# Running 16 early expert tiles between the pieces of the second image's routing, in a two-layer MetaFormer kernel

## The chip, the cores and the metric

The kernel runs on one core of a Trainium2 chip. The time is the device time of one execution in microseconds (us). An execution of the program also leaves a profile: the busy time of each engine, the waits between them, and the clock that TensorE was granted. In the profile PE is TensorE, PEld its weight loads, DVE VectorE, ACT ScalarE, POOL GpSimd and SP SyncE, which here issues most DMAs. L784 means line 784 of the kernel.

## What is computed

The input is two images of 256 channels and 56 x 56 pixels. Two layers follow one another, each a token mixer and a mixture of experts with a residual around both. Layer 0 mixes by 7 x 7 window attention, layer 1 by two ternary 3 x 3 convolutions with batch normalisation over both images. The part that matters here is layer 1 after its convolutions:

```python
x = x + relu(out1 + out2)             # out2: second convolution, normalised over both images
t = tokens(x)                         # 2 * 56 * 56 = 6272 tokens of 256 numbers
n = layer_norm(t)
logits = n @ gate_w + gate_b          # 8 experts
top2_vals, top2_idx = top_k(softmax(logits), 2)
for each expert e:                    # 256 -> 512 -> 256
    y = gelu(n @ W1[e] + b1[e]) @ W2[e] + b2[e]
    acc += weight of e for the token * y
x = t + acc
```

All of it is float32, and the output has the shape of the input.

## The kernel before

Each image is cut into 7 strips of 8 pixel rows, 448 tokens each; STRIPS lists the 14 of them, image 0's first. A strip's tokens are held as 4 groups of 112 tokens.

**Routing of layer 1.** `residual(i)` loads the strip's kept input (`back`), adds the two convolutions' results on DVE (L2071), rectifies on ACT (L2074), turns the strip from channels to tokens with 8 PE transposes (L2083) and adds `back` on DVE (L2087). `norm` takes the mean and variance per token on DVE (L705, L707), a square root on ACT (L712), scales into `u` on ACT (L726), turns `u` back with 8 PE transposes (`pu`, L770) and two ACT copies (`ut`, L775), and multiplies by the gate (`pl`, 16 matmul records, L784). `settle` takes a batch of one or two strips: it finds each token's two best experts by some 15 small DVE steps (L811 to L860) with a rank count on PE (`rk`, L843 to L846), which gives each token a row in its expert's stretch of a table `xs` in DRAM. POOL then scatters the tokens there, one indirect DMA for 112 tokens and one of the two choices (L870), so 8 for a strip. All these functions are generators, and `in_order` advances them step by step, so that two or three strips are under way at once. DVE, PE, ACT and SP take their work in the order in which it is written there; POOL's is not in that hand-written order.

**Tiles.** An expert's rows are worked off in tiles of 256 rows. `tiles(part)` computes on DVE, from the counts, which expert and rows each tile has. Part 0 holds tiles that are known to be full once the first FIRST[1] = 10 strips are placed: EARLY[1] = (2 * 448 * 10 - 8 * 255) // 256 = 27 of them. Part 1 holds the other full tiles, 41 full ones in all, and part 2 the 23 half tiles of 128 rows. From the ninth place on (MIX = 8) half tiles are mixed among the full ones. The early tiles' rows may be read while late strips are still being scattered; `fence` makes SP wait until the early ones are written.

**The expert loop.** `experts_in_order` runs over 64 tiles j. SP issues the rows of tile j + 4 and the weights of tile j + 3 (1154 KB). `turn(j + 2)` transposes rows on PE (L1073) and copies them on ACT (L1077). `first(j + 1)` makes 4 PSUM tiles `ph` (L1105), each followed by a Gelu on ACT (L1112). `second(j)` makes `py` (L1122), DVE adds the bias into `y` (L1130), and POOL scatters the tile's rows into `ys` (L1132), two indirect DMAs for a full tile. `gates`, the softmax weights of all tokens, is advanced by one step after each tile.

In the kernel before, `in_order` runs all 14 strips, and only then the loop starts its first tile:

```python
plan, n_full = tiles(1, in_order(), True)
plans1.append(plan)
plans1.append(tiles(2, n_full, True))
nc.sync.value_load(fences[0])
route_ps.close()
...
experts1.send((tp1, ps1))
```

Behind the expert loop the two rows of each token are gathered from `ys`, weighted and added, and the result is turned back to channels.

Layer 0 has the same two parts. There the loop over tiles already runs beside the routing of the last four strips, by a function `beside` that is called once per tile.

Of the kernel before, what the change touches and what calls it, by code (L numbers as in the profile page):

```python
# [10 lines left out]
F32 = mybir.dt.float32  # L11
# [44 lines left out]
NEVER = -3e38  # L56
U_BUFS = (4, 6)

# [574 lines left out]
def metaformer(ctx: ExitStack, tc: tile.TileContext, a: dict, out: bass.AP, flag):  # L633
# [3 lines left out]
    dram = ctx.enter_context(tc.tile_pool(name="dram", bufs=3, space=DRAM))  # L637

    def disjoint(inst, group, others):
# [96 lines left out]
    def routing(layer, wp, tp, ps):  # L736
# [18 lines left out]
        def norm(i, src, late=False):  # L755
# [20 lines left out]
            if layer == 0:  # L776
                eng.tensor_tensor(src, src, u, ALU.add)
                nc.sync.dma_start(x_mid[i], src)
                yield
            lg = lgs[:, i * NTT : (i + 1) * NTT, :]  # L780
            pl = ps.tile([TT, NTT, E], F32, tag="pl" if layer else "aux", name="pl")
            for t in range(NTT):
# [239 lines left out]
    def experts_in_order(layer, FF, plans, ys, wp, at_tile):  # L1022
# [13 lines left out]
        live = {}  # L1036

        def planned(j):
# [27 lines left out]
        def turn(j):  # L1066
            d = live[j]
            _, held, name, n = planned(j)
            gp = blocks_of(j)
            pt = ps.tile([P, KC, G], F32, tag="pt", name="pt", bufs=2 if layer else 1)  # L1070
            for k in range(KC):
                for i in range(gp):
                    nc.tensor.transpose(  # L1073
                        pt[:, k, i * P : (i + 1) * P], d["xg"][:, i, k * P : (k + 1) * P], ident
                    )
            d["ut"] = tp.tile([P, KC, G], F32, tag="ut", name="ut")
            nc.scalar.copy(d["ut"][:, :, : gp * P], pt[:, :, : gp * P])  # L1077
# [73 lines left out]
        for j in range(len(tiles)):  # L1151
# [66 lines left out]

    BATCHES = [[0], [1], [2], [3], [4, 5], [6, 7], [8, 9], [10, 11], [12, 13]]

# [94 lines left out]
    with ExitStack() as st:  # L1315
# [324 lines left out]
        x_all = None  # L1640
        X, XT, pad, sums = {}, {}, [], []
        mid = ctx.enter_context(ExitStack())
        pads = mid.enter_context(ExitStack())
        wq_held = ExitStack()

        def routed_all():
# [21 lines left out]

            cp = pads.enter_context(tc.tile_pool(name="pads", bufs=1, reuse_waits="tile"))
            for b in range(B):  # L1670
                t = cp.tile([P, HC, KC, WC], F32, tag=f"pad{b}", name=f"pad{b}")
# [3 lines left out]
                nc.gpsimd.memset(t[:, 1 : HC - 1, :, WC - 1 : WC], 0.0)  # L1675
                pad.append(t)
            mid.enter_context(wq_held)
# [32 lines left out]
    with mid:  # L1710
# [336 lines left out]
        with ExitStack() as both:  # L2047
# [9 lines left out]
            route_ps = ExitStack()  # L2057
            ps = route_ps.enter_context(
                tc.tile_pool(name="route_ps1", bufs=2, space=PSUM, reuse_waits="tile")
            )  # L2060

            def residual(i):

                b, s = STRIPS[i]
                r = X[b, s]
                nr = tp.tile([P, KC, NT], F32, tag="nr", name="nr")
                back = tp.tile([TT, NTT, C], F32, tag="back", name="back")
                nc.sync.dma_start(back, x_mid[i])
                for o in range(KC):
# [9 lines left out]
                    )  # L2079
                pt = ps.tile([TT, NTT, C], F32, tag="pt", name="pt")  # L2080
                for t in range(NTT):
                    for k in range(KC):
                        nc.tensor.transpose(  # L2083
                            pt[:, t, k * P : (k + 1) * P], nr[:, k, t * TT : (t + 1) * TT], ident
                        )
                yield
                nc.vector.tensor_tensor(XT[b, s][:TT], pt, back, ALU.add)  # L2087

# [11 lines left out]

            def in_order():


                n = len(STRIPS)
                jobs = {}
                ready = iter(())
                for i in range(n + 2):
# [3 lines left out]
                    finish(ready)  # L2111
                    if not plans1 and FIRST[1] - 1 in sent:
                        plan, n_early = tiles(0)
                        plans1.append(plan)
                        fence()
                    if young == 0:
                        next(jobs[young])
                    if i < n:
                        jobs[i] = strip(i)
                        next(jobs[i])  # L2120
                        if i == n - 1:

                            next(experts1)
                    if young > 0 and young in jobs:
# [19 lines left out]
            experts1 = experts_in_order(1, 2 * C, plans1, ys[1], wp1, lambda j: next(gating, None))  # L2144
            with tc.manual_schedule(engines=ENGINES):
                plan, n_full = tiles(1, in_order(), True)
                plans1.append(plan)
                plans1.append(tiles(2, n_full, True))

                nc.sync.value_load(fences[0])  # L2150

                route_ps.close()
                pads.close()
                tp1 = both.enter_context(tc.tile_pool(name="moe_t1", bufs=2, reuse_waits="tile"))
                ps1 = both.enter_context(
                    tc.tile_pool(name="moe_ps1", bufs=2, space=PSUM, reuse_waits="tile")
                )
# [133 lines left out]
```

## Time and profile before

| | us |
|---|---|
| median of 3 runs | 1854.04 |
| lowest and highest run | 1850.1, 1854.89 |
| the profiled execution | 1852.05 |
| its span (what the profile covers) | 1850.1 |
| PE busy | 1530.3 (83%) |
| DVE busy | 979.4 (53%) |
| ACT busy | 696.1 (38%) |
| POOL busy | 655.1 (35%) |

Times in the views are counted from the span's start. The layer 1 routing begins at about 1182 us and the first expert tile's second half at about 1399; the last stage, from about 1780 on, gathers and writes out. A view by windows gives the busy time of each engine in a stretch, the clock granted to PE as a share of full speed, and the DMA's share and rate. In a list of waits, the engine named behind the arrow is the one whose signal came last; "remote" and "another core or an unknown queue" mean that the profile found no engine of the core for it. In a timeline each line is one instruction or a run of like ones: start, duration, engine, line, operation, and in brackets the idle time before it and what ended that.

### The profile page before, as it was taken

Reading aid. Unit: us, or ns where it says so; the run is one execution under the profiler, and the core shown is the slowest. Engines: PE = TensorE matmul, PEld = TensorE weight load, DVE = VectorE, ACT = ScalarE, POOL = GpSimd, SP = SyncE. Lnnn points to the kernel's source line nnn. Section 1 sums busy time; section 2 is a strip of 40 time slices with the busy share of each in tenths; the row PEclk is TensorE's granted clock in tenths of the full one; section 3 lists DMA queues with packets and bytes.
Section 4 is the critical chain, followed back from the end, with each engine's and each line's share of the span. In section 5 each row is a group of like instructions: output and inputs, shape, how many; then the busy total and the mean of one; then the engine's idle time right before and its main releaser. Section 6 shows DMA issues by size and latency. Waiting matters only on the chain.

```text
span 1850.1 us, 25838 instructions
## 1 busy us (share of the span) xinstructions
PE 1530.3 (83%) x8612; PEld 1199.4 (65%) x8612; DVE 979.4 (53%) x2688; ACT 696.1 (38%) x1358; POOL 655.1 (35%) x664
## 2 busy tenths in 40 slices
PE   6999998999778669894899799666348999999963
PEld 3555555555467557783788688555337888888842
DVE  4467566465645337845999788666432111111136
ACT  3454442434333324643444532344213333333312
POOL 3112534335333654442344143164562222222210
PEclk9999988999889879995999899755558999999975
DMA  7022333213267667885551000133544778788758
GB/s 244 22 83 82 113 90 112 62 52 93 60 205 229 230 208 263 307 256 156 158 163 53 1 1 1 40 112 98 170 136 152 270 265 270 262 279 277 274 161 301
DMA packets 91886, 291.77 MB, mean 158 GB/s; under 512 B 20487, under 2 KB 35803, under 8 KB 80416
## 3 DMA queue, kind: packets, MB, share of 16 engines
q1 hardware_dynamic: 66736, 231.79, 40.5%
q0 software_dynamic: 21200, 51.82, 8.0%
q10 hardware_dynamic: 3808, 6.42, 1.0%
q8 instruction: 70, 1.15, 0.3%
q14 instruction: 72, 0.59, 0.1%
HBM read 218.51 MB, written 74.20 MB: 158 GB/s over the span
## 4 chain that ended last, share of the span: by engine, by line
PE 52%; DVE 21%; DMA 8%; issue 7%; another core or an unknown queue 5%; POOL 4%; ACT 3%; SPq 0%; POOLq 0%; ACTq 0%; DVEq 0%
PE ph L1105 14%; PE py L1122 12%; PE av L1486 5%; PE sc L1457 3%; PE pj L1409 3%; DVE x L1191 3%; PE pw L1556 3%; PE pv L1431 3%; PE pl L784 2%; PE pt L1073 2%; DMA got<-ys 2%; DMA out<-o_out 2%; DVE oc L1543 2%; DVE t_stats L705 2%
## 5 line engine op out<-in xcount | busy, mean ns | idle before, releaser
L1105 PE MATMUL ph<-ut,w 128*128 128x256 f32 (+1 forms) x1472 | 320.3, 370 | 28.2 <-issue 20.3
L1130 DVE TENSOR_TENSOR y<-py,w 128x512 f32<-128x512 f32 (+1 forms) x120 | 76.8, 640 | 439.2 <-PE py L1122 379.2
L1122 PE MATMUL py<-w,h 128*128 128x256 f32 x1288 | 298.8, 380 | 0.0
L1105 PEld LDWEIGHTS ph<-ut,w 128*128 128x128 f32 x1472 | 258.2, 200 | 59.8 <-issue 22.4
L870 POOL DMA_INDIRECT xs<-u,pos x224 | 217.1, 969 | 168.0 <-issue 87.0
L1122 PEld LDWEIGHTS py<-w,h 128*128 128x128 f32 x1288 | 244.8, 192 | 33.1
L1132 POOL DMA_INDIRECT ys<-y,dest x136 | 136.3, 1003 | 274.8 <-DVE dest L1080 185.5
L1112 ACT ACTIVATE h<-ph,w 128x256 f32<-128x256 f32 (+1 forms) x368 | 162.3, 447 | 131.2 <-PE ph L1105 82.2
L1476 ACT ACTIVATE ex<-sc 112x476 f32<-112x476 f32 (+3 forms) x224 | 116.7, 570 | 207.8 <-PE sc L1466 174.9
L1077 ACT COPY ut<-pt 128x512 f32<-128x512 f32 (+1 forms) x120 | 65.2, 543 | 302.5 <-PE pt L1073 244.9
L1486 PE MATMUL av<-ex,vals 112*64 112x238 f32 (+3 forms) x896 | 124.1, 397 | 17.8 <-DVE acc L1496 14.3
L1792 PE MATMUL pc<-lo,wq 128*128 128x448 f32 x336 | 132.2, 395 | 6.5 <-DVE lo L1767 6.4
L1496 DVE TENSOR_TENSOR acc<-av,acc 128x238 f32<-128x238 f32 (+3 forms) x224 | 87.8, 407 | 87.5 <-PE av L1486 65.3
L1792 PE MATMUL pc<-hi,wq 128*128 128x448 f32 x336 | 131.7, 394 | 2.0 <-DVE x L1816 1.8
L1132 POOL DMA_INDIRECT ys<-y,to x81 | 82.3, 1016 | 135.0 <-DVE dest L1080 76.4
L1191 DVE SCALAR_TENSOR_TENSOR x<-got,wgt,x 112x256 f32<-112x256 f32 x216 | 102.3, 544 | 30.4 <-DMA got<-ys 30.4
L1935 PE MATMUL pc<-hi,wq 128*128 128x448 f32 (+1 forms) x288 | 104.4, 371 | 15.9 <-ACT hi L1902 9.4
L1935 PE MATMUL pc<-lo,wq 128*128 128x448 f32 (+1 forms) x288 | 103.6, 368 | 0.2 <-DVE lo L1903 0.2
L1457 PE MATMUL sc<-q_im,keys 32*112 32x238 f32 (+3 forms) x896 | 94.3, 427 | 9.5 <-ACT ex L1476 5.7
L1486 PEld LDWEIGHTS av<-ex,vals 112*64 112x64 f32 x896 | 55.9, 141 | 67.7 <-issue 25.2
L1765 POOL TENSOR_TENSOR v<-pad 128x928 f32<-128x928 f32 (+1 forms) x28 | 56.4, 2028 | 99.4 <-DVE lo L1767 49.1
L1073 PE MATMUL pt<-ident,xg 128*128 128x128 f32 x434 | 71.7, 287 | 15.5 <-ACT ut L1077 10.4
(273 smaller groups left out, 2479.7 us busy)
## 6 DMA issues: line engine op xcount, KB each, us to landing
w<-in_L_experts SPq DMA_DIRECT2D x64, 1154.0 KB
w<-in_L_experts SPq DMA_DIRECT2D x56, 641.0 KB
xg<-xs SPq DMA_DIRECT2D x97, 260.0 KB
got<-ys SPq DMA_DIRECT2D x28, 896.0 KB
acc<-in_fresh SPq DMA_DIRECT2D x14, 896.0 KB
xt<-in_x_tok SPq DMA_DIRECT2D x14, 448.0 KB
xr<-in_x_tok SPq DMA_DIRECT2D x14, 448.0 KB
rec<-shares SPq DMA_DIRECT2D x28, 224.0 KB
```

Source lines behind the costliest of these rows:

```text
L870: w = nc.gpsimd.indirect_dma_start(xs[:, :], bass.IndirectOffsetOnAxis(ap=pos[:, j, t0 + t : t0 + t + 1], axis=0), us[t // NTT][:, t % NTT ...
L1073: nc.tensor.transpose(pt[:, k, i * P : (i + 1) * P], d["xg"][:, i, k * P : (k + 1) * P], ident)
L1105: nc.tensor.matmul(ph[:, :g], w1[:, k, f * P : (f + 1) * P], d["ut"][:, k, :g], start=k == 0, stop=k == KC - 1,)
L1112: nc.scalar.activation(d["h"][:, f, :g], ph[:, :g], AF.Gelu, bias=b1[:, f : f + 1])
L1122: nc.tensor.matmul(py[:, i, :], d["h"][:, f, i * P : (i + 1) * P], w2[:, f, :], start=f == 0, stop=f == NF - 1,)
L1132: o = nc.gpsimd.indirect_dma_start(ys[:, :], bass.IndirectOffsetOnAxis(ap=d["to"][:, i : i + 1], axis=0), y[:, i, :], None, bounds_check=T ...
L1191: nc.vector.scalar_tensor_tensor(xt[:, t, :], y[:, t, j, :], wgt[:, j, n : n + 1], xt[:, t, :], ALU.mult, ALU.add)
L1457: nc.tensor.matmul(sc[h // 2][:, h % 2, :nq], keys[g][p, c, tx * TT : (tx + 1) * TT], q_im[p, c, r0:r1, c0:c1], start=True, stop=False,)
L1476: nc.scalar.activation(e[:, :, :nq], sc[j][:, :, :nq], AF.Exp, scale=HD**-0.5)
L1486: nc.tensor.matmul(av[VW * i : VW * (i + 1), :nq], vals[g % 3][:, tx, 2 * c + j, 2 * i : 2 * i + 2, :].rearrange("p a d -> p (a d)"), ex[j ...
L1792: nc.tensor.matmul(pc[:, :NT], wq[:, k, c, dx * C + o * P : dx * C + (o + 1) * P], part[:, :, k, dx : dx + W], start=m == 0, stop=m == 2 * ...
L1935: nc.tensor.matmul(pc[:, : 2 * ns * W], wq[:, k, c, dx * C + o * P : dx * C + (o + 1) * P], part[:, : 2 * ns, k, dx : dx + W], start=m == ...
```

## The change

FIRST[1] goes from 10 to 7, so part 0 is what image 0 fills: EARLY[1] = (2 * 448 * 7 - 8 * 255) // 256 = 16 tiles. `in_order` is split. `early_strips` runs strips 0 to 6 as before, plans part 0 and sets the fence. Then the expert loop starts, and `late_strips`, a generator, runs strips 7 to 13 in small steps, 9 to a strip, which `beside1` takes between the parts of each tile: 2 before `first(j + 1)`, 2 between it and `second(j)`, and 3 after. When its steps are used up, or at the latest after tile 11, parts 1 and 2 are planned. Half tiles are mixed in from the 17th tile on, nearly one to one with the full ones.

To have both under way, PSUM is shared: while the strips run, the routing has 2 banks for all its PSUM tiles (`aux`), and the loop has 1 for `pt`, 3 for `ph` and 2 for `py`; afterwards the loop gets 2, 4 and 2 as before. In late strips the result of the transposes (L2083) is held in two halves, and the add (L2087) is made in two. In SBUF image 0's pad is given up before the tiles start, so the pads become two pools; `nr` has one buffer instead of two and `u` 5 instead of 6. The batches of `settle` are arranged so that none spans both images.

```diff
-U_BUFS = (4, 6)
+U_BUFS = (4, 5)
-FIRST = (10, 10)
+FIRST = (10, 7)
-MIX = 8
...
-                tiles.insert(MIX + q + (NFULL - MIX) * q // NHALF, (2, q))
+                tiles.insert(n0 + q + (NFULL - n0) * q // NHALF, (2, q))
...
-            pt = ps.tile([P, KC, G], F32, tag="pt", name="pt", bufs=2 if layer else 1)
+            pt = ps.tile([P, KC, G], F32, tag="pt", name="pt", bufs=2 if wide(ps) else 1)
...
-                ph = ps.tile([P, 512], F32, tag="ph", name="ph", bufs=4 if layer else 3)
+                ph = ps.tile([P, 512], F32, tag="ph", name="ph", bufs=4 if wide(ps) else 3)
...
+            if layer:
+                at_tile(j, 0)
             if j + 1 < len(tiles):
                 first(j + 1)
+            if layer:
+                at_tile(j, 1)
             second(j)
             if at_tile is not None:
-                at_tile(j)
+                at_tile(*((j, 2) if layer else (j,)))
...
-    BATCHES = [[0], [1], [2], [3], [4, 5], [6, 7], [8, 9], [10, 11], [12, 13]]
+    BATCHES = [[0], [1], [2], [3], [4, 5], [6], [7, 8], [9, 10], [11, 12], [13]]
...
-                nr = tp.tile([P, KC, NT], F32, tag="nr", name="nr")
+                nr = tp.tile([P, KC, NT], F32, tag="nr", name="nr", bufs=1)
...
-                nc.vector.tensor_tensor(XT[b, s][:TT], pt, back, ALU.add)
+                xt = XT[b, s][:TT]
+                for at, pt in halves:
+                    nc.vector.tensor_tensor(xt[:, at], pt, back[:, at], ALU.add)
...
+            def late_strips():
+
+                sending = iter(())
+                young = None
+                for i in range(FIRST[1], len(STRIPS) + 1):
+                    job = strip(i) if i < len(STRIPS) else iter(())
+                    steps = iter(())
+                    for q in BATCHES:
+                        if q[-1] == i - 1 and i > FIRST[1]:
+                            steps = settle(q)
+                    for at in range(9):
+                        if at in (0, 2, 3):
+                            next(job, None)
+                        if at in (1, 4, 5) and young is not None:
+                            next(young, None)
+                        if at == 5:
+                            next(job, None)
+                        if at >= 6:
+                            next(steps, None)
+                        next(sending, None)
+                        yield
+                    for _ in sending:
+                        yield
+                    sending, young = steps, job
+                for _ in sending:
+                    yield
...
+            def beside1(j, part):
+                nonlocal route
+                if route is None:
+                    if part == 2:
+                        next(gating, None)
+                    return
+                done = object()
+                for _ in range((2, 2, 3)[part]):
+                    if next(route, done) is done:
+                        break
+                else:
+                    if j < EARLY[1] - ROWS_AHEAD - 1 or part < 2:
+                        return
+                    for _ in route:
+                        pass
+                route = None
+                plan, n_full = tiles(1, n_early, True)
+                plans1.append(plan)
+                plans1.append(tiles(2, n_full, True))
+                late_ps.close()
...
+            experts1 = experts_in_order(1, 2 * C, plans1, ys[1], wp1, beside1)
+            route = late_strips()
             with tc.manual_schedule(engines=ENGINES):
-                plan, n_full = tiles(1, in_order(), True)
-                plans1.append(plan)
-                plans1.append(tiles(2, n_full, True))
-
+                n_early = early_strips()
+                next(experts1)
                 nc.sync.value_load(fences[0])
```

More of the change, by code (lines that the diff above doesn't have):

```diff
@@ L637, in metaformer, with __init__, tile @@
     dram = ctx.enter_context(tc.tile_pool(name="dram", bufs=3, space=DRAM))
+    class Banks:
+        def __init__(self, pool, wide=False):
+            self.pool, self.wide = pool, wide
+        def tile(self, *args, **kw):
+            return self.pool.tile(*args, **kw)
     def disjoint(inst, group, others):
@@ L779, in norm @@
                 yield
+            elif i >= FIRST[1]:
+                yield
             lg = lgs[:, i * NTT : (i + 1) * NTT, :]
-            pl = ps.tile([TT, NTT, E], F32, tag="pl" if layer else "aux", name="pl")
+            pl = ps.tile([TT, NTT, E], F32, tag="pl" if layer and ps.wide else "aux", name="pl")
             for t in range(NTT):
@@ L1036, in experts_in_order, with wide @@
         live = {}
+        def wide(ps):
+            return isinstance(ps, Banks) and ps.wide
         def planned(j):
@@ L1640, in metaformer @@
         x_all = None
-        X, XT, pad, sums = {}, {}, [], []
+        X, XT, pad, sums = {}, {}, {}, []
         mid = ctx.enter_context(ExitStack())
-        pads = mid.enter_context(ExitStack())
+        pads = [mid.enter_context(ExitStack()) for _ in range(B)]
         wq_held = ExitStack()
@@ L1667, in routed_all @@
                 X[b, s] = x_all[:, i, : KC * NT].rearrange("p (k n) -> p k n", n=NT)
-            cp = pads.enter_context(tc.tile_pool(name="pads", bufs=1, reuse_waits="tile"))
-            for b in range(B):
+            for b in reversed(range(B)):
+                cp = pads[b].enter_context(
+                    tc.tile_pool(name=f"pads{b}", bufs=1, reuse_waits="tile")
+                )
                 t = cp.tile([P, HC, KC, WC], F32, tag=f"pad{b}", name=f"pad{b}")
@@ L1675, in routed_all @@
                 nc.gpsimd.memset(t[:, 1 : HC - 1, :, WC - 1 : WC], 0.0)
-                pad.append(t)
+                pad[b] = t
             mid.enter_context(wq_held)
@@ L2057, in metaformer @@
             route_ps = ExitStack()
-            ps = route_ps.enter_context(
-                tc.tile_pool(name="route_ps1", bufs=2, space=PSUM, reuse_waits="tile")
+            ps = Banks(
+                route_ps.enter_context(
+                    tc.tile_pool(name="route_ps1", bufs=2, space=PSUM, reuse_waits="tile")
+                ),
+                True,
             )
@@ L2079, in residual @@
                     )
-                pt = ps.tile([TT, NTT, C], F32, tag="pt", name="pt")
+                if i >= FIRST[1]:
+                    yield
+                halves = []
                 for t in range(NTT):
+                    if i < FIRST[1] and not t:
+                        pt = ps.tile([TT, NTT, C], F32, tag="pt", name="pt")
+                        halves.append((slice(0, NTT), pt))
+                    elif i >= FIRST[1] and not t % 2:
+                        pt = ps.tile([TT, 2, C], F32, tag="aux", name="pt")
+                        halves.append((slice(t, t + 2), pt))
+                    at = halves[-1][0].start
                     for k in range(KC):
                         nc.tensor.transpose(
-                            pt[:, t, k * P : (k + 1) * P], nr[:, k, t * TT : (t + 1) * TT], ident
+                            pt[:, t - at, k * P : (k + 1) * P],
+                            nr[:, k, t * TT : (t + 1) * TT],
+                            ident,
                         )
                 yield
-                nc.vector.tensor_tensor(XT[b, s][:TT], pt, back, ALU.add)
+                xt = XT[b, s][:TT]
+                for at, pt in halves:
+                    nc.vector.tensor_tensor(xt[:, at], pt, back[:, at], ALU.add)
             def strip(i):
@@ L2099, in fence, with early_strips @@
                 fences.append(some)
-            def in_order():
-                n = len(STRIPS)
+            def early_strips():
+                n = FIRST[1]
                 jobs = {}
@@ L2111, in in_order @@
                     finish(ready)
-                    if not plans1 and FIRST[1] - 1 in sent:
-                        plan, n_early = tiles(0)
-                        plans1.append(plan)
-                        fence()
                     if young == 0:
@@ L2120, in in_order @@
                         next(jobs[i])
-                        if i == n - 1:
-                            next(experts1)
                     if young > 0 and young in jobs:
@@ L2139, in in_order @@
                 finish(ready)
-                return n_early
+                plan, n_early = tiles(0)
+                plans1.append(plan)
+                fence()
+                return n_early
+            def late_strips():
[19 more added lines that the diff above has]
+                    for _ in sending:
+                        yield
+                    sending, young = steps, job
+                for _ in sending:
+                    yield
@@ L2142, in metaformer @@
             plans1, fences = [], []
             gating = gates()
-            experts1 = experts_in_order(1, 2 * C, plans1, ys[1], wp1, lambda j: next(gating, None))
-            with tc.manual_schedule(engines=ENGINES):
-                plan, n_full = tiles(1, in_order(), True)
+            def beside1(j, part):
[15 more added lines that the diff above has]
+                plan, n_full = tiles(1, n_early, True)
@@ L2147, in metaformer @@
                 plans1.append(plan)
                 plans1.append(tiles(2, n_full, True))
+                late_ps.close()
+                ps1.pool = late_ps.enter_context(
+                    tc.tile_pool(name="moe_ps1", bufs=2, space=PSUM, reuse_waits="tile")
+                )
+                ps1.wide = True
+            experts1 = experts_in_order(1, 2 * C, plans1, ys[1], wp1, beside1)
+            route = late_strips()
+            with tc.manual_schedule(engines=ENGINES):
+                n_early = early_strips()
+                next(experts1)
@@ L2150, in metaformer @@
                 nc.sync.value_load(fences[0])
                 route_ps.close()
-                pads.close()
+                pads[0].close()
+                late_ps = both.enter_context(ExitStack())
+                ps.pool = late_ps.enter_context(
+                    tc.tile_pool(name="late_ps1", bufs=2, space=PSUM, reuse_waits="tile")
+                )
+                ps.wide = False
                 tp1 = both.enter_context(tc.tile_pool(name="moe_t1", bufs=2, reuse_waits="tile"))
-                ps1 = both.enter_context(
-                    tc.tile_pool(name="moe_ps1", bufs=2, space=PSUM, reuse_waits="tile")
+                ps1 = Banks(
+                    late_ps.enter_context(
+                        tc.tile_pool(name="early_ps1", bufs=2, space=PSUM, reuse_waits="tile")
+                    )
```

## The prediction

> **What bounds the kernel now.** I first cut the stretch that the change touches into windows by stage (columns: window, its length, then busy us and instruction count of PE, PEld, DVE, ACT and POOL, granted clock, DMA share, GB/s). The last two lines are stages of layer 0, read as models.
>
> ```profile
> core 0: us, PE busy (x) PEld busy (x) DVE busy (x) ACT busy (x) POOL busy (x), PEclk, DMA share, GB/s
> 1182.00:1285.00 103.00, 62.24 (x314) 54.13 (x314) 65.28 (x272) 40.80 (x82) 47.80 (x48) 0.52 0.36 104
> 1285.00:1350.00 65.00, 32.96 (x166) 29.32 (x166) 36.52 (x149) 20.83 (x43) 32.15 (x34) 0.50 0.51 160
> 1350.00:1394.00 44.00, 16.80 (x69) 13.66 (x68) 11.85 (x58) 4.62 (x8) 29.19 (x31) 0.58 0.34 110
> 1452.00:1600.00 148.00, 148.00 (x812) 132.49 (x811) 22.40 (x74) 55.84 (x130) 40.34 (x41) 1.00 0.81 272
> ...
> 585.00:685.00 100.00, 70.05 (x350) 59.07 (x349) 38.54 (x147) 28.69 (x56) 62.16 (x64) 0.88 0.67 219
> 720.00:830.00 110.00, 99.66 (x484) 85.90 (x484) 79.74 (x198) 53.76 (x100) 52.00 (x51) 0.95 0.83 274
> ```
>
> Layer 1's routing (1182 to 1394) leaves PE idle for 38 to 62% of its windows at a clock of 0.50 to 0.58; its experts (from 1399) are PE alone, 148 of 148 us at 1.00. Putting tiles into the routing's gaps looks worth much. Next, in the chain of waits, the end of the routing:
>
> ```profile
> 1352.61 15.98 another core or an unknown queue
> ...
> 1379.62 9.28 another core or an unknown queue
> ...
> 1398.95 3.45 PE py L1122 x16
> ...
> 1402.84 3.46 PE ph L1105 x16
> 1406.29 3.45 PE py L1122 x16
> ```
>
> The first second half of a tile (py) starts at 1398.95; from there a full tile takes 7.34 us (1402.84 to 1410.18). In front of it lie waits of no named cause. The list of waits and the timeline show what they go with:
>
> ```profile
> ACT ut L775 <- remote: 46.2, 5, 12.9
> ```
> ```profile
> 1302.73 0.79 PE L846 MATMUL rk<-hots,all_w 112*112 112x56 bf16 x7
> 1303.38 0.99 PE L770 MATMUL pu<-ident,u 112*128 112x112 f32 x4
> ...
> 1308.78 0.94 POOL L870 DMA_INDIRECT xs<-u,pos  x1 [0.30 <-issue]
> 1312.59 0.53 ACT L775 COPY ut<-pu 128x448 f32<-128x448 f32 x1 [12.87 <-remote]
> ```
>
> PE's transposes are done at 1304.4, yet ACT, which waits for them alone, goes on at 1312.59, after POOL's row of scatters (L870, one each 1.25 us, 16 from 1289.7) has ended. The same happens after 10 to 20 scatters in a row: 1229 to 1240, 1273 to 1285, 1352 to 1389. I call it a freeze; the profile names no cause, but PE, ACT, DVE and SP all stop in it. It went with 0.65 to 0.8 scatters per us, not with the 51 POOL instructions in 110 us of the last window above.
>
> **Part by part.** The change is worth what follows from three numbers: when experts start, how long the mixed stage lasts, and how much tile work is then done.
>
> *Earlier start.* FIRST 10 to 7 gives (2 x 448 x 7 - 8 x 255) // 256 = 16 early tiles. Routing stops after strip 6. In the timeline strip 5's logits are added at 1253.43; strip 6, with no strip behind it, follows by 1262, its places by 1267. POOL's scatters of strips 4 and 5 start at about 1259 and those of 6 join on: 24 x 1.25 = 30 us, to 1289. Before, the last scatter ahead of the fence ended at 1334.0 and SP issued the first rows at 1341.92, 7.9 us later; so rows go at 1297. Plan and the first three weight loads (12.6 us for three at 1322.7) lie beside the scatters: nothing, or up to 8 us if the plan's DVE steps are frozen, as they were from 1364 on. Rows 3 us, transposes, copy and one first half at half clock (6.05 us, the 16 matmuls at 1369) and a second: py of tile 0 at about 1315, against 1398.95. **84 us earlier** (75 to 90).
>
> *Length of the mixed stage.* late_strips gives 9 steps for each of 7 strips and 9 to end, and some 5 for the last scatters: 77, at 7 per tile 11.1 tiles. PE's own work: 11.1 x 7.34 = 82 us, and per strip 8 pt transposes (1.2, twice the 0.60 us of four at clock 1.00), 8 pu (1.2), 16 pl (1.74 at 264.98) and the rank matmuls (0.6): 4.7 x 7 = 33. Together 115. What is lost on top:
> - Square roots. L712 stays on ACT, now between Gelus. Layer 0 shows one:
>
> ```profile
> 598.07 1.28 ACT L712 ACT_TABLE_LOAD   x1
> 602.76 0.30 ACT L712 ACTIVATE t_rstd<-t_mv,eps 112x4 f32<-112x4 f32 x1 [3.40 <-DVE t_mv L707]
> 603.55 1.28 ACT L1112 ACT_TABLE_LOAD   x1
> 603.58 0.66 PE L1073 MATMUL pt<-ident,xg 128*128 128x128 f32 x4 [1.54 <-ACT ut L1077]
> ```
>
> ACT is held from 598.07 to 604.8. py went 596.26, 600.15, 606.34: 6.19 where a tile takes 3.89, so 2.3 us lost. 7 x 2.3 = 16.
> - Order. Five of the seven steps of a tile lie together with only 0.6 us of tile work between (after second, before first). There rank waits for DVE's step before it (about 3 us, L811 to L833 at 1298.4 to 1301.8) and pl and pt wait for DVE and ACT to clear the two aux banks (1.22 us, L2087; two copies of 0.53). Laid out by hand over nine tiles I lose 1 to 2 us per strip: 10. With ph in 3 banks and pt in 1, the fourth ph waits for one Gelu (0.47) with 2.6 us to spare: nothing while ACT is free.
> - Freezes. The 16 scatters of two strips come out in 8 steps, 1.1 tiles, with 2 or 3 of ys between: some 23 us of unbroken POOL. About 7 us of PE lost for each of three, 23 with the last strip. Bounds: none (the 720 to 830 window), or the 11 us of each pair seen now and 30 us for the last four strips, 50.
> - Clock. 0.88 in the layer 0 model; 6 us. If 0.5 comes back after freezes, 20.
>
> 16 + 10 + 23 + 6 = 55: 115 + 55 = **170 us**, a PE share of 0.68. The layer 0 window, the nearest row, has 0.70, which gives 164. I take 169, nearer to the itemised sum, since layer 0 has no PE order as tight as this.
>
> The Trainium skill ("ScalarE: Activation LUTs", What ACT_TABLE_LOAD costs) speaks against the change: a switch is about 1.28 us of load and 1.38 us of drain, and unlike functions should be batched. The 14 switches would be 37 us of ACT by it and the total 20 us worse if none of it hid; the row above holds load, drain and wait together. The skill ("SBUF — State Buffer", two separate sides) says that PE and ACT never wait for the port that GpSimd shares; by that a freeze would cost nothing and the total be 23 us better. The timeline above disagrees.
>
> *Work done.* 82 us of tiles need not be run later. So the path grows by 169 - 82 = 87 and starts 84 earlier.
>
> *Handover.* After the last step tiles(1) and tiles(2) go onto DVE in one piece (some 45 steps, about 12 us unfrozen); y of the next tile waits behind them, py has two banks of 7 us, so little of it shows. Rows of tile 16 wait on SP for the late scatters, with the weights of tile 15 queued behind; both are needed two tiles, 15 us, later. New PSUM pool: one drain. **4 us** (0 to 15).
>
> *Half tiles later.* From the 17th on they alternate almost one to one with full ones. A pair moves 2 x 1154 KB of weights, 390 KB of rows and 393 KB of ys in 11.09 us: 278 GB/s against 272 now, with 340 to 408 GB/s seen at 750 to 770. PE never waits there now: nothing (to 8 us if 272 is near the limit).
>
> *Small ones.* The add of L2087 in two halves, two pads, nr in one buffer and u in five: each had its reader done long before (u of strip i - 5 is sent 20 us earlier): nothing.
>
> Sum: -84 + 87 + 4 + 0 = **+7 us**. The profiled execution took 1852.05 us (span 1850.1), 2 below the median of 1854.04: 1859.
>
> **Rivals.** *Scatters thin out (faster).* As steps follow PE's pace, no more than 8 or 10 scatters run unbroken, and freezes go as in the 720 to 830 window; clock stays at 1. Then 115 + 26 = 141: 141 - 82 = 59 and -84 + 59 + 4 = -21, 1831; with the start at its early end (90) and 3 of the handover gone, 1822. It decides once freezes and clock cost under 16 us together instead of 29: then the time is 0.3% below before's. For it: POOL's total is 78 scatters x 1.26 = 98 us in 170. Against: they come in packs of 16.
>
> *POOL sets the pace (much slower).* The last 24 scatters run into one freeze as the last 32 did (1352 to 1394), rows of tile 16 come late: 20 us more freeze and 10 of handover, 1889.
>
> *Weights bound the half tiles.* If 278 GB/s isn't reached beside half tiles, 8 us over the forecast: 1867, and PE waits for w appear after tile 16.
>
> **How the numbers follow.** About 0.3%, 5.6 us, is what a measurement can tell from no change. Forecast, 0.50: of it 0.07 faster, 0.13 within, 0.30 slower. Scatters thin out: 0.30, faster. POOL sets the pace: 0.13; weights: 0.07, both slower. Faster 0.37, same 0.13, slower 0.50. The range goes from the lower rival's end, 1822, to just short of the heaviest, 1885, which leaves out some 0.2. The forecast's own range is 1843 to 1878.
>
> **What would show it.** Right: first py near 1315; the route's scatters in packs of 16 or more, ACT or DVE "remote" waits of 5 us or more at the end of each; 14 table loads more; PE share about 0.7 from there to tile 11; then dense PE at 1.00. Wrong: no remote waits in the mixed stage, or a stage under 150 us (then faster), or PE waits for xg or w after tile 16.

## The result, and the profile after

The changed kernel takes 1880.27 us (1877.35 to 1885.03), the kernel before beside it 1854.47 us (1850.1 to 1859.32): a ratio of 1.0141 [1.0108, 1.0174], slower by 26 us. The profiled execution of the changed kernel took 1885.03 us with a span of 1883.2, against 1852.05 and 1850.1, so the two traces differ by 33 us. The file has grown: L726 is now L733, L775 L782, L793 L802, L870 L879, L1073 L1085, L1077 L1089, L1105 L1117, L1112 L1124, L1122 L1134, L1130 L1142, L1132 L1144, L2087 L2121.

The tile part is framed by the row of `py` from the first tile's start to the last's (count, then least, median and greatest ns, first and last start, shapes). Before, then after:

```profile
L1122 PE MATMUL py<-w,h x840: 379/379/382, 1398.8 to 1777.4; 128*128 128x256 f32 x168
```
```profile
L1134 PE MATMUL py<-w,h x840: 379/379/634, 1311.4 to 1808.5; 128*128 128x256 f32 x168
```

Tile 0 starts 87.4 us earlier; from the first `py` to the last it takes 497.1 us instead of 378.6, which is 118.5 more; the end behind that takes 2.0 more (74.7 against 72.7). -87.4 + 118.5 + 2.0 = +33.1, the difference of the spans. So the whole loss lies in the tile part, and the windows show where in it (same columns as above):

```profile
core 0: us, PE busy (x) PEld busy (x) DVE busy (x) ACT busy (x) POOL busy (x), PEclk, DMA share, GB/s
1182.00:1296.00 114.00, 52.26 (x259) 45.59 (x259) 58.72 (x262) 31.81 (x63) 55.10 (x57) 0.50 0.35 109
1272.80:1298.20 25.40, 0.00 (x0) 0.00 (x0) 0.00 (x0) 0.00 (x0) 13.90 (x16) 0.50 0.68 221
1316.00:1508.00 192.00, 121.97 (x616) 102.45 (x615) 54.64 (x224) 70.05 (x125) 73.08 (x77) 0.79 0.41 138
1508.00:1640.00 132.00, 131.47 (x719) 117.36 (x718) 32.21 (x122) 51.22 (x117) 36.09 (x37) 1.00 0.80 269
```

From 1508 on PE is busy 131.47 of 132 us at full clock: nothing is lost there. In the mixed stage, 1316 to 1508, PE is busy 0.64 of the time at a clock of 0.79. And there is a line that nothing before had: for 25.4 us ahead of tile 0 PE, ACT and DVE do not execute one instruction, while POOL issues the last 15 scatters ahead of the fence, and the fence's own transfer.

The starts of `py` show the mixed stage tile by tile. In us, from tile 0 to tile 11: 10.8, 12.8, 16.6, 16.4, 26.8, 13.7, 30.2, 16.7, 16.0, 30.1, 8.2; together 198.1. Three tiles are twice as long as their neighbours. The timeline of the second shows why (start, duration, engine, line; a cut of it):

```profile
1415.50 0.93 POOL L879 DMA_INDIRECT xs<-u,pos  x1 [0.30 <-issue]
1416.33 2.84 PE L1117 MATMUL ph<-ut,w 128*128 128x256 f32 x12
...
1417.10 0.57 ACT L1089 COPY ut<-pt 128x512 f32<-128x512 f32 x1
...
1419.21 0.93 POOL L879 DMA_INDIRECT xs<-u,pos  x1 [0.30 <-issue]
1420.45 0.98 POOL L1144 DMA_INDIRECT ys<-y,dest  x1 [0.30 <-issue]
...
1431.69 0.94 POOL L879 DMA_INDIRECT xs<-u,pos  x1 [0.30 <-issue]
1432.36 0.19 DVE L802 TENSOR_TENSOR lgs<-pl,gate_b 112x32 f32<-112x32 f32 x1 [15.18 <-remote]
1432.47 0.17 DVE L722 RECIPROCAL t_rstd<-t_rstd 112x4 f32<-112x4 f32 x1
1432.67 0.16 DVE L723 TENSOR_TENSOR t_nmr<-t_nmr,t_rstd 112x4 f32<-112x4 f32 x1
1432.87 2.07 ACT L733 ACTIVATE u<-x,t_nmr,t_rstd 112x256 f32<-112x256 f32 x4 [15.20 <-issue]
```

POOL's row of 18 scatters runs from 1410.55 to 1432.63. PE's last matmul ends at 1419.2, the matmuls (`pl`) that DVE waits for had been done since 1416.5, and DVE goes on at 1432.36: the freeze of the prediction, now beside tiles. The list of waits from 1300 to 1520 has the freezes of all three long tiles (a cut of it):

```profile
DVE lgs L802 <- remote: 31.4, 2, 16.2
...
ACT ut L1089 <- remote: 20.4, 1, 20.4
...
DVE y L1142 <- remote: 18.2, 1, 18.2
```

### The profile page after: what moved, and what is told of

Its sections match the earlier page's. It is cut to its first block, busy times and chain, and to the rows that moved or that the text cites. A ratio compares the mean times of both kernels' runs of the same rounds, so it can differ in the third digit from the quotient of the medians.

```text
span 1883.2 us, 25864 instructions
## 1 busy us (share of the span) xinstructions
PE 1520.2 (81%) x8613; PEld 1186.9 (63%) x8613; DVE 980.7 (52%) x2714; ACT 711.6 (38%) x1372; POOL 652.8 (35%) x664
## 5 line engine op out<-in xcount | busy, mean ns | idle before, releaser
L1117 PE MATMUL ph<-ut,w 128*128 128x256 f32 (+1 forms) x1472 | 327.3, 374 | 42.4 <-ACT h L1124 33.1
L1117 PEld LDWEIGHTS ph<-ut,w 128*128 128x128 f32 x1472 | 261.8, 203 | 78.0 <-ACT h L1124 35.8
L1142 DVE TENSOR_TENSOR y<-py,w 128x512 f32<-128x512 f32 (+1 forms) x120 | 76.8, 640 | 445.7 <-PE py L1134 368.7
L1134 PE MATMUL py<-w,h 128*128 128x256 f32 x1288 | 301.8, 383 | 0.0
L879 POOL DMA_INDIRECT xs<-u,pos x224 | 214.8, 959 | 173.5 <-issue 76.9
L1134 PEld LDWEIGHTS py<-w,h 128*128 128x128 f32 x1288 | 246.1, 193 | 33.5
L1144 POOL DMA_INDIRECT ys<-y,dest x136 | 136.7, 1005 | 311.8 <-DVE dest L1092 128.7
L1124 ACT ACTIVATE h<-ph,w 128x256 f32<-128x256 f32 (+1 forms) x368 | 161.2, 447 | 129.7 <-PE ph L1117 90.3
L1089 ACT COPY ut<-pt 128x512 f32<-128x512 f32 (+1 forms) x120 | 65.0, 542 | 304.2 <-PE pt L1085 252.9
L1144 POOL DMA_INDIRECT ys<-y,to x81 | 82.0, 1012 | 130.0 <-DVE dest L1092 75.8
L1085 PE MATMUL pt<-ident,xg 128*128 128x128 f32 x434 | 73.1, 290 | 45.8 <-DMA xg<-xs 34.9
L1085 PEld LDWEIGHTS pt<-ident,xg 128*128 128x128 f32 x434 | 57.2, 151 | 71.4 <-DMA xg<-xs 33.6
```

The source lines that it names most:

```text
L879: w = nc.gpsimd.indirect_dma_start(xs[:, :], bass.IndirectOffsetOnAxis(ap=pos[:, j, t0 + t : t0 + t + 1], axis=0), us[t // NTT][:, t % NTT ...
L1085: nc.tensor.transpose(pt[:, k, i * P : (i + 1) * P], d["xg"][:, i, k * P : (k + 1) * P], ident)
L1117: nc.tensor.matmul(ph[:, :g], w1[:, k, f * P : (f + 1) * P], d["ut"][:, k, :g], start=k == 0, stop=k == KC - 1,)
L1124: nc.scalar.activation(d["h"][:, f, :g], ph[:, :g], AF.Gelu, bias=b1[:, f : f + 1])
L1134: nc.tensor.matmul(py[:, i, :], d["h"][:, f, i * P : (i + 1) * P], w2[:, f, :], start=f == 0, stop=f == NF - 1,)
L1144: o = nc.gpsimd.indirect_dma_start(ys[:, :], bass.IndirectOffsetOnAxis(ap=d["to"][:, i : i + 1], axis=0), y[:, i, :], None, bounds_check=T ...
```

## The experiments

They came in four sets, each on one chip with the kernel before beside it, and the sets differ in a way that turned out to be the best experiment of all. Each set ran on another chip. The kernel before took 1760.06 us in the first set, 1856.66 in the second, 1758.34 in the third and 1857.66 in the fourth. Where it is near 1760, no trace of any kernel has a "remote" wait; where it is near 1857, all have them. Only ratios within a set are compared below, and traces of the same level.

**First set (kernel before 1760.06): four ways to break up the packs, or the order.**

*Strips settled singly.*

```diff
-    BATCHES = [..., [6], [7, 8], [9, 10], [11, 12], [13]]
+    BATCHES = [..., [6], [7], [8], [9], [10], [11], [12], [13]]
```

> Edit: strips 7 to 12 of the changed kernel are settled one by one instead of in pairs, so a pack has 8 scatters instead of 16. Theory A (packs): the changed kernel's loss beyond the forecast is the three freezes in the mixed stage, which packs of 16 scatters bring about; the three frozen tiles took 26.8, 30.2 and 30.1 us where the other seven took 14.7 on average, 43 us in all. Packs of 8 stay under the 10 scatters after which the freezes set in: no waits of ACT or DVE over 8 us in the mixed stage, 43 us back less some 3 for more DVE steps, so 1838 to 1848 us, faster than the kernel before. Theory B (order): the loss lies in PE's waits for DVE and ACT in the hand-written order (rank counts, square roots with their table switches), and the long gaps are those waits: settling one by one doubles the number of rank waits, so 1880 to 1890 us.

Measured: 1791.02 us, ratio 1.0188 [1.0152, 1.0225]. With nothing frozen in this set, the size of the packs could not be tested. But the loss was there without any freeze.

*Singly, and a step after each scatter.*

```diff
+                    if layer and strips[0] >= FIRST[layer] and not j:
+                        yield
                 yield
```

> Edit: as e1_single, and each of the 8 scatters of a late strip is given a step of its own, so that they are spread over 8 of 9 steps. Theory A: at most 2 or 3 scatters unbroken, so no freeze at all; 0 to 6 us better than e1_single, 1835 to 1845 us. Theory B: as e1_single, 1880 to 1890 us. If e1_single still shows freezes and this kernel none, the length of a pack decides and 8 is already too many.

Measured: 1806.68 us, 1.0263 [1.0235, 1.0292]. The stretch from first to last `py` is 460.7 us against 452.5 of the first: more steps, a longer mixed stage, and what is left over is run in one piece at tile 13 (an interval of 16.5 us where the first has 7.3). The other 10.5 us by which this trace is later, at tile 0, come from ahead of the edit: layer 0's last `py` is at 806.9 against 795.5.

*Without the square roots of the late strips (the root is left out of their normalisation).*

```diff
-            nc.scalar.activation(rstd, mv[:, :, 1], AF.Sqrt, bias=eps[:TT])
+            nc.scalar.activation(rstd, mv[:, :, 1], AF.Identity if root == "late" else AF.Sqrt, bias=eps[:TT])
```

> Edit: in the changed kernel the square root on ACT of the 7 late strips' norm is left out (Identity takes its place, on the same operands), so that ACT changes no table in the mixed stage; each token's logits get a positive factor, so the choice of experts and the tiles stay as they are. Theory A: only the 7 square roots' own cost goes, 7 x 2.3 = 16 us, freezes stay: 1860 to 1868 us. Theory B: ACT's table switches are the main loss, 14 loads and the order around them: 1850 us or less, and the long gaps shrink.

Measured: 1786.2 us, 1.0158 [1.0131, 1.0185]. `py` of tiles 0 to 11 takes 144.2 us; the changed kernel on the third set, the same level, takes 153.2. So the seven roots cost 9 us (the next run, of this set, has the changed kernel's layer 1 and takes 153.6). Without them the stage looks like this:

```profile
1269.30:1413.50 144.20, 121.37 (x648) 104.02 (x647) 60.14 (x242) 53.95 (x115) 69.01 (x73) 0.91 0.55 183
```

*A filler on POOL after each late scatter.*

```diff
+                    if layer and strips[0] >= FIRST[layer]:
+                        nc.gpsimd.tensor_tensor(minus_half, ones[:TT, :NTT], minus_half, ALU.pow)
```

> Edit: in the changed kernel POOL does a small power of about 1.05 us (a step that feeds nothing) after each late scatter, so scatters follow each other after some 2.4 us instead of 1.24, in packs of the same 16. Theory A, rate: freezes come from 0.8 scatters per us; at 0.4 they vanish, some 40 us back, 1835 to 1850 us, unless POOL itself gets late with ys. Theory A, count: freezes come once 10 scatters or so stand in one pack; a pack now lasts 38 us, so they last longer, 1900 us and more. Theory B: POOL is not in it, 1878 to 1885 us.

Measured: 1843.27 us, 1.0484 [1.0452, 1.0516]. It did not test what it was meant to: POOL's order isn't written by hand, and all 56 fillers ran in layer 0. The timeline of POOL:

```profile
507.83 61.23 POOL L887 TENSOR_TENSOR minus_half<-ones,minus_half 112x4 f32<-112x4 f32 x56
```

There they held up the scatters, and with them layer 0's tiles: PE waits 41.85 us for rows there. Its layer 1 is therefore the changed kernel's, with packs of 18, 20 and 28 and nothing frozen: 451.7 us from first to last `py`.

**Second set (kernel before 1856.66): both kernels again, and two changes of size.**

*The changed kernel, unaltered.*

> The changed kernel unaltered, beside the kernel before and the other three of this call on one chip. The four runs so far were on a chip on which the kernel before took 1760.06 us instead of 1854.47, and their traces have no stretch in which PE, ACT and DVE all stand still behind a pack of scatters. Theory A (the stands-still behind the packs, 43 us of the mixed stage, are the excess loss): on a chip without them the ratio to the kernel before is at most 1.00, or with them 1.014 again. Theory B (the order of the steps, PE's waits on DVE and ACT and the lower clock are enough): without stands-still the ratio is still 1.015 to 1.025, since the variants with single strips and without square roots gave 1.019 and 1.016 there.

Measured: 1883.85 us, 1.0118 [1.0072, 1.0163]; the first trace again (tile 0 at 1316.2, 499.9 us of tiles, 25.5 us of standstill ahead of them).

*The kernel before, unaltered.*

> The kernel before unaltered, for its trace beside the changed kernel's on the same chip. Theory A: where the time is near 1760 the waits for another core or an unknown queue, which are on the chain of the routing stage of the first profile, are gone, and that stage (from the end of the convolution at about 1182 to py(0) at 1399 there) is the part that is shorter, by the most of the 94 us. Theory B: all stages are shorter by a common share, 5 per cent, as from a higher granted clock.

One execution, 1866.1 us. Not the level that the expectation spoke of; as in its first trace there are stretches of 4 to 7 us without PE, ACT and DVE in the routing, and tile 0 at 1408.7.

*Twice as many steps per tile.*

```diff
-                for _ in range((2, 2, 3)[part]):
+                for _ in range((4, 4, 6)[part]):
```

> The changed kernel with (4, 4, 6) steps of the late routing per tile in place of (2, 2, 3): the mixed stage has 5.5 tiles instead of 11, each with 14 steps. Theory A (the loss belongs to the strips: their packs, square roots and scatters): the loss is the same per strip, the time stays within 5 us of the changed kernel. Theory B (the loss belongs to the order, a tile that lies between two steps covers their waits): with twice the steps to a tile less work covers each wait, the time is 10 to 25 us above the changed kernel.

Measured: 1895.37 us, 1.0163 [1.0107, 1.0219], whose interval overlaps the changed kernel's. In the traces the tile part is no longer (495.9 against 499.9 us), though the strips now lie over five or six tiles. But the first steps already run ahead of the first `py`, and from tile 0's first transposes to it 21.2 us pass instead of 12.9; counted from those transposes to the last `py` it is 517.2 against 512.7. By these two traces, 4.5 us, theory A's 5 holds: what is lost belongs to the strips, not to the tiles beside them. The medians are 11.5 us apart, which fits theory B; with the intervals overlapping, that stays undecided.

*The kernel before with single strips.*

```diff
-    BATCHES = [[0], [1], [2], [3], [4, 5], [6, 7], [8, 9], [10, 11], [12, 13]]
+    BATCHES = [[i] for i in range(14)]
```

> The kernel before with every strip settled singly in place of pairs from strip 4 on: packs of 8 scatters for layer 1, with more settling steps. Theory A: on a chip with stands-still the packs of 8 have none and the kernel gains 15 to 30 us; on one without it is within 5 us. Theory B: five more settlements per layer with their small instructions cost 5 to 15 us wherever it runs.

Measured: 1868.87 us, 1.0058 [1.0027, 1.0089], no gain. POOL put the scatters of neighbouring strips together again (16 from 1356.2 to 1375.8, for one), and the freezes stayed: DVE waits 49.3 us for "remote" in five pieces. The batch does not set the size of a pack here, so whether packs of 8 freeze was not tested.

**Third set (kernel before 1758.34): where the loss lies without freezes.** In this set tile 0 of the changed kernel is preceded by the same standstill as in every other trace of it, so the experiments give it something to cover it: strips 7 and 8, or 7 to 10, are routed ahead of tile 0 again, while the plan still rests on strips 0 to 6.

```diff
+LATE = FIRST[1] + 2        # and + 4 in the second
 ...
-                n = FIRST[1]
+                n = LATE
 ...
                     finish(ready)
+                    if not plans1 and FIRST[1] - 1 in sent:
+                        plan, n_early = tiles(0)
+                        plans1.append(plan)
+                        fence()
 ...
-                finish(ready)
-                plan, n_early = tiles(0)
-                plans1.append(plan)
-                fence()
+                finish(ready)
 ...
-                for i in range(FIRST[1], len(STRIPS) + 1):
+                for i in range(LATE, len(STRIPS) + 1):
```

> The changed kernel with strips 7 and 8 routed as before, ahead of tile 0 and beside the plan and the fence; strips 9 to 13 are mixed in. In the changed kernel PE, ACT and DVE stand still for 25.5 us ahead of tile 0 in every trace (1277.9 to 1303.4 in the last one), on both chips so far, while POOL issues the last 24 scatters and the fence lands; the kernel before has other strips to route there and stands still 4 to 7 us at most. Theory C (the loss of 22 to 34 us against the kernel before is that stretch, and a strip costs the path the same mixed or ahead of tile 0): the stretch is gone, py(0) comes within 10 us of the changed kernel's, and the ratio to the kernel before is 0.995 to 1.005. Theory D (a mixed strip costs more than one ahead of tile 0; the stretch is only moved): a standstill of 15 us or more remains ahead of tile 0, and the ratio is 1.008 or more.

> The same with strips 7 to 10 ahead of tile 0 and 11 to 13 mixed in. Theory C: the time is within 6 us of the kernel with strips 7 and 8 ahead, since two strips fewer in the mixed stage (each some 16 us over the tiles) are two more ahead of tile 0 (some 14 to 16 each). Theory D: it is 10 us or more faster than that one.

> The changed kernel once more, on the chip of the two kernels above. Where the kernel before takes near 1855 here: 1.011 to 1.017 times it, with two or three stretches of 13 to 16 us in the mixed stage. Where it takes near 1760, and there are none: Theory A (they are the loss) says 1.00 or less, theory C says a loss of 20 to 35 us as before, 1.012 to 1.02.

Measured:

| | us | ratio to the kernel before | tile 0 at | first to last `py` |
|---|---|---|---|---|
| all 7 mixed in (the changed kernel) | 1799.04 | 1.0215 [1.0189, 1.0241] | 1274.2 | 451.4 |
| 5 mixed in | 1775.18 | 1.0098 [1.0079, 1.0117] | 1270.6 | 428.5 |
| 3 mixed in | 1760.14 | 1.0017 [0.9999, 1.0036] | 1277.3 | 412.0 |

The changed kernel loses 41 us where nothing freezes, more than where it does, and more than the 20 to 35 of theory C. The ratio lies in the 1.015 to 1.025 that theory B of the second set gave for runs without freezes, so a loss of this size needs none. Its windows: the standstill ahead of tile 0, the mixed stage from tile 0 to tile 11, and one pack of 18 scatters.

```profile
1236.70:1262.30 25.60, 0.00 (x0) 0.00 (x0) 0.03 (x1) 0.00 (x0) 13.95 (x16) 0.50 0.62 221
1274.20:1427.00 152.80, 124.43 (x646) 105.34 (x645) 59.79 (x241) 71.96 (x129) 68.01 (x71) 0.89 0.51 172
1322.20:1344.30 22.10, 18.47 (x89) 16.05 (x90) 5.66 (x20) 11.89 (x22) 16.91 (x18) 0.81 0.59 200
```

The same row for a pack of 18 in the first trace after (the freeze shown above):

```profile
1410.55:1432.63 22.08, 8.32 (x56) 6.99 (x54) 4.12 (x15) 3.02 (x5) 16.90 (x18) 0.75 0.55 178
```

POOL works 16.9 us in both. PE works 18.47 us beside the one and 8.32 beside the other. So a pack by itself does not stop PE; something that comes with the level does.

The standstill is another thing. Its waits, in the changed kernel of this set from 1236 to 1275:

```profile
ACT ut L1089 <- PE pt L1085: 39.8, 2, 38.6
PEld pt L1085 <- DMA xg<-xs: 30.9, 1, 30.9
PE pt L1085 <- DMA xg<-xs: 30.8, 1, 30.8
```

PE has nothing to do until tile 0's rows (`xg`) land, and these wait for the fence behind POOL's last 24 scatters (1224.6 to 1254.3 here, then the fence at 1256.89 and the rows at 1259.42). With strips 7 to 10 ahead of tile 0 no stretch without PE, ACT and DVE of over 4 us is left there, and PE starts the tiles beside a pack that has 36 scatters:

```profile
1256.30:1277.30 21.00, 16.73 (x84) 14.56 (x83) 6.15 (x28) 9.01 (x17) 16.09 (x17) 0.66 0.79 244
```

Four strips more ahead of tile 0 make it start only 3.1 us later, and take 39.4 us out of the tile part. The 3.1 flatters them: layer 0, which these edits do not touch, ended 6.9 us earlier in that trace (its last `py` at 804.6 against 811.5), so counted from there the four cost 10.0 us, 2.5 each. Strips 7 and 8 alone leave 10.1 us of the standstill and 17 of the 41 us.

By the numbers theory D did better: 1.0098 with two strips, and 15.0 us less with four. It is also right that a mixed strip costs more than one of these four: 9.9 us each in the tile part, and 11.1 for each of the last three (412.0 less 378.6). But the reason is theory C's. What is left of the standstill is less than the 15 us that D asked for; with four strips it is gone, and the loss with it. And the last three strips, which have no standstill to fill, cost some 9 us each ahead of tile 0 in the kernel before (an estimate: 1305, worked out below, less 1277.3), nearly as much as among the tiles. C's fault was to hold two strips for cover enough. Theory A fell: with no freeze at all the change is still slower.

**Fourth set (kernel before 1857.66): the standstill alone, put into the kernel before.**

```diff
-                    if not plans1 and FIRST[1] - 1 in sent:
-                        plan, n_early = tiles(0)
-                        plans1.append(plan)
-                        fence()
 ...
-                            next(experts1)
 ...
                 finish(ready)
+                plan, n_early = tiles(0)
+                plans1.append(plan)
+                fence()
+                next(experts1)
                 return n_early
```

> The mirror of the last three: the kernel before, nothing mixed in, with plan, fence and the first fetch of weights put behind the last of its 14 strips, so that tile 0 has nothing to cover them, as in the changed kernel. Theory C (a tile 0 whose scatters, plan, fence and rows nothing covers costs the path 25 to 40 us by itself): a stretch of 15 to 30 us appears ahead of tile 0 with PE waiting for xg, and the kernel is 20 to 40 us above the kernel before, with no step of the routing beside a tile. Theory D (mixed strips are the loss, the uncovered stretch costs little): it is at most 10 us above it. Its PE has no tile work in the routing, so py(0) on a chip where the kernel before takes near 1760 also gives that kernel's: theory C says 1300 to 1310 for the kernel before, worked out as 1758 less 449 for its tiles and its end.

Measured: 1862.05 us, 1.0027 [1.0001, 1.0053]: 4 us, where theory C said 20 to 40. The stretch is there (a window of this kernel), and its PE waits 17.59 us for `xg` in it:

```profile
1375.00:1395.00 20.00, 0.19 (x1) 0.10 (x1) 6.19 (x30) 0.00 (x0) 8.90 (x10) 0.50 0.57 190
```

But at this level the kernel before has little cover to lose. The same end of its routing in the first profile:

```profile
1355.00:1399.00 44.00, 16.64 (x58) 13.00 (x58) 16.17 (x81) 5.94 (x12) 25.43 (x27) 0.59 0.25 75
```

Tile 0's first matmul is at 1361 there, and then it stood, with short breaks, behind 32 scatters until 1389. In the kernel of this run PE waits behind the same 32 scatters first, and then for the rows:

```profile
1377.94 0.19 PE L920 MATMUL counts<-seen_all,all_w 112*128 112x8 bf16 x1 [21.19 <-remote]
1395.72 1.12 PE L1073 MATMUL pt<-ident,xg 128*128 128x128 f32 x4 [17.59 <-DMA xg<-xs]
```

So the standstill takes the place of the later part of a freeze, and costs nearly nothing. What theory C says is therefore shown for the level without freezes only. That the routing of strips 7 to 10 ahead of tile 0 also wins the loss back at the level of the prediction was not run.

## Why the prediction was right, and where it was off

It said slower by 5 us at 1859, with a range of 1822 to 1885; measured is slower by 26, at 1880.27, near the upper end of the range and 2 us above the forecast's own (1843 to 1878). In the terms of its sum, the trace has -87.4 for -84 (start), 198.1 less 11 x 7.34, which is 117.4, for 87 (mixed stage less the tiles done in it), 1.1 for 4 (handover and half tiles), and 2.0 for an end that it took as unchanged. The two levels, put side by side, tell what each term was worth. The kernel before has no trace at the upper level; its tile 0 there is an estimate, 1758.34 less 2 (time less span in the profiled executions), 378.6 and 72.7, which is 1305.

| us | before, freezes | after, freezes | before, none | after, none |
|---|---|---|---|---|
| tile 0 starts at | 1398.8 | 1311.4 | 1305 (estimate) | 1274.2 |
| first to last `py` | 378.6 | 497.1 | 378.6 (taken over) | 451.4 |
| of that, tile 0 to tile 11 | | 198.1 | | 153.2 |

- **Earlier start: right.** 1311.4 where 1315 was said, 87.4 earlier where 84 was. The 25 us standstill is inside that number; the prediction had its scatters, fence and rows in the sum, as times that follow one another. What it did not ask is what covered them before, and so what it would take to cover them again.
- **Length of the mixed stage: the step that failed.** 198.1 us for 11 tiles, where 170 was said for 11.1. PE's own work, roots, order and clock came to 147 in the sum, and the stage takes 153 where nothing freezes: 6 off. But two of its terms were off, each the other way: the roots cost 9 where 16 was said, and the order some 23 where 10 was. In the run without roots PE is busy 121.37 us, as the sum's 115 and 6 for the clock say, and idle for 22.8.
- **The term that was mis-sized is the freezes:** 23 us said, 198.1 - 153.2 = 45 measured, near the end of its bounds (50). The 45 are the difference of two traces of different sets, and hold what the lower clock costs beside a freeze. Three packs of 16 were foreseen, and they came; 7 us of PE were allowed for each. The three long tiles (26.8, 30.2, 30.1) take 15.6, 14.2 and 13.6 in the trace without freezes: 11 to 17 us each.
- **Clock.** 0.88 was said and is 0.89 without freezes; with them 0.79.
- **Handover, half tiles, small ones: right**, or a little dear (4 said, 1.1 measured). `py` of tiles 11 to 13 come 7.3 us apart; from 1508 PE is busy 131.47 of 132 us with half tiles alternating, so the rival of the weights is out.
- **Of the rivals,** scatters that thin out got the stage without freezes, in two sets, but not its reason: packs of 18 to 28 scatters stand there. And the change was slower still (1.0215): the rival's fault is the start, 31 us earlier instead of 84, because the kernel before is rid of its freezes too. POOL as the pace-setter did not come: tile 16 did not wait for rows.
- **The 23 us of the skill's page** ("SBUF — State Buffer", two separate sides, by which PE and ACT never wait for the port that GpSimd shares) against the row of the first trace: PE works through a pack at the one level (18.47 of 22.1 us) and stops at the other (8.32 of 22.08). That the stops are waits for that port no run shows.
- **The table loads** (the Trainium skill, "ScalarE: Activation LUTs", What ACT_TABLE_LOAD costs): the loads are 1.28 us each in these traces as on the page, 14 of them; but the page's 37 us of ACT came to 9 us of the path; the rest does not show in it.

So the direction was right, for a reason that holds only in part. The freezes are not what the change costs: they took as much from the kernel before, or somewhat more. From the kernel before it is the 94 us by which tile 0 comes later, less the 24 to 32 that layer 0 had by then (its last `py` is at 835.6, against 811.5, 804.6 and 803.7 in the traces of the third set): 62 to 70, in the routing, an estimate like the 1305. From the changed one it is 12 us ahead of tile 0, counted likewise, and 46 in the tile part: 58. The change moves the freezes with the scatters. What it costs without them is plain: seven strips in the tiles cost 72.8 us, 10.4 each, and their absence ahead of tile 0 gives back 31, because four of them had lain in the shadow of the last scatters, the plan, the fence and the rows, where they cost 3.1 by the start of tile 0, or 10.0 counted from the end of layer 0. With those four put back the loss is gone. No version beat the kernel before; the one with three strips mixed in equals it.

Open: what stops the engines at the one level and not at the other, and what sets the level; as each set ran on another chip, chip and time can't be told apart. Whether the 26 us at the level with freezes divide in the same way was not separated there.

## What to carry to other kernels

Before work is moved into the gaps of another stage, ask what it covers where it is now. Here four of the seven strips hid a chain of scatters, fence and loads that someone has to wait for anyway; they cost 1 to 2.5 us each there, and 10 each beside the tiles. And where idle time ahead of a stage has no named cause, it may travel with the instructions that it goes with: a gain counted from a trace with such stops must carry them along to the new place.

## What was not expected of the hardware

- The same kernel has two levels: 1854 to 1858 us in three sets of runs, 1758 to 1760 in two, the runs of a set within 1% of its median. At the lower speed there are stretches of 4 to 16 us in which PE, ACT and DVE stand still behind scatters, with waits of up to 21 us for "remote"; at the higher there is no such wait.
- The stops go with scatters in a row, and yet the scatters do not make them by themselves: 18 in 22.1 us leave PE busy 18.47 us at one level and 8.32 us at the other, with POOL busy 16.9 us in both.
- The granted clock follows the work: 0.79 in the mixed stage with freezes, 0.89 without, 0.50 in the standstill of 25.4 us, 1.00 where tiles run alone.
